# A selective-scan layer: who spreads dt * x, and which operand of each tile's scan lies in PSUM

## The chip, the cores and the metric

The kernel runs on one core of a Trainium2 chip. A core has five engines that run side by side, each with its own queue of instructions that it takes in order: TensorE (PE, matrix multiply, writes to PSUM only), VectorE (DVE, elementwise work and scans), ScalarE (ACT, activations and copies), GpSimd (POOL, here elementwise work in SBUF only), and SyncE (SP, which here issues all DMAs). SBUF is the working memory, PSUM the small memory of eight banks that PE writes. The metric is the device time of one execution of the whole program in microseconds (us), lower is better.

## The reference

The network has four layers. Layers 0, 2 and 3 are deformable convolutions; layer 1 is a "VSS" block, whose core is a two-dimensional selective scan (SS2D) in four directions. Only layer 1 is touched. Cut to its core (B images, K = 4 directions, 256 channels d, 16 states n, L = 56 x 56 positions):

```python
dt = softplus(einsum('bkrl,kdr->bkdl', dts, dt_projs_w) + dt_projs_b)
A = -exp(A_logs).reshape(K, Di, N)
def step(h, t):
    dt_t, u_t, B_t, C_t = t
    h = h * exp(dt_t[..., None] * A) + (dt_t * u_t)[..., None] * B_t[:, :, None, :]
    y = einsum('bkdn,bkn->bkd', h, C_t)
    return (h, y)
_, ys = scan(step, h0, (dt, xs, Bsm, Csm))
```

So for every channel and state there is a recurrence over the positions: the old state times a decay exp(dt * A), plus dt * x * B, and the result weighted with C is summed over the states.

## The kernel before

Layer 1 is the class `Vss`. Its method `scans` takes 8 images x 4 directions x 4 chunks of 784 positions, 128 steps in all. A step has 32 tiles of 128 partitions x 784 positions: a tile holds 32 channels x 4 states on its partitions. Tiles are ordered by channel group `cg` (8 of them) and, inside one, by state group `sg` (4), so four tiles in a row share the channels, and with them dt and dt * x. A step and a tile within it are `at` and `t`; `t % 4` is `sg`. There are 4,096 tiles in all.

For each tile:

- `fetch_dt` (L1286, once for a channel group) and `fetch_row` (L1278) bring dt, dt * x, and the rows of B and C into SBUF by DMA from SP's queue, repeated over the partitions.
- `spread` (L1335, once for a channel group) has PE multiply dt * x with the identity, in two halves of 392 positions, which puts a copy of it into PSUM: the tile `dtu`, two banks, one buffer.
- `decay` (L1343): ACT computes dA = exp(dt * A) into PSUM, two buffers of two banks.
- `inputs` (L1348): u = dt * x * B. For the first three tiles of a group DVE multiplies `dtu` (PSUM) with B (SBUF) into SBUF, tag `u`, two buffers. For the fourth (`on_pool`) POOL does it from SBUF to SBUF, tag `up`.
- L1449: DVE's `tensor_tensor_scan` runs the recurrence over the 784 positions into `h` (SBUF, three buffers); its start value is one column of `st`. For one of its inputs it reads dA in PSUM, for the other u in SBUF.
- L1452: ACT copies the last column of h back into `st` for the next chunk, 32 tiles later (not after the last chunk).
- L1454: POOL multiplies h with C into `hc` (SBUF, six buffers).
- `add_sums` (L1372): PE sums `hc` over the states into `acc` (one PSUM bank), two tiles at a time. `open_sums` (L1364) starts `acc` with the skip term or the running sum over the directions, `close_sums` (L1380) has ACT copy it out (L1389), once for two channel groups.

PSUM's eight banks are `misc` 1, `dtu` 2, dA 4, `acc` 1.

The loop at L1405 walks over the tiles. At tile `now` it emits the decay and the u of tile `now + 1` (the u of a fourth tile one tile earlier), at the second tile of a channel group the spread of the next group (L1442, tile `now + 3`), then the scan, the column copy and POOL's product of tile `now`. Sums are held back: `add_sums` by three tiles, opening and closing by five. Between the tiles `advance` and `ready` emit small pieces of background work: `prepare` (projections, softplus of the next step), `input_stage` (normalization and convolution of the next image) and `output_stage` (norms, gate, MLP of finished rows). They use the single `misc` bank, where PE and ACT take turns.

A planner (the tile framework) assigns the buffers, inserts the waits and orders each engine's queue by its own estimate of when things become ready, so the queue may differ from the order of emission. `issue_after(x)` puts what is emitted inside it behind instruction x on the same engine's queue. Before the change the sums are so tied behind the last spread (L1374).

Of the kernel before, what the change touches and what calls it, by code (L numbers as in the profile page):

```python
# [41 lines left out]
F32 = mybir.dt.float32  # L42
BF16 = mybir.dt.bfloat16
I32 = mybir.dt.int32
AF = mybir.ActivationFunctionType
ALU = mybir.AluOpType
AX = mybir.AxisListType
PSUM = bass.MemoryType.PSUM
# [70 lines left out]
SC, SR = 784, 14  # L119
NSC = L // SC  # L120
SH = SC // 2
# [11 lines left out]
TC, TS = 32, 4  # L133
NCG, NSG = DI // TC, NST // TS
# [342 lines left out]
class Dcn:  # L477
# [9 lines left out]
    def run(self):  # L487
        tc, nc = self.tc, self.nc
        with ExitStack() as ctx:
            enter = ctx.enter_context  # L490
            self.cp = enter(tc.tile_pool(name="c_const", bufs=1))
            self.img = enter(tc.tile_pool(name="c_img", bufs=1))
            self.fp = enter(tc.tile_pool(name="c_front", bufs=1))
            self.up = enter(tc.tile_pool(name="c_unit", bufs=1))
            self.bp = enter(tc.tile_pool(name="c_block", bufs=3))
            self.tp = enter(tc.tile_pool(name="c_tail", bufs=1))
            self.pt = enter(tc.tile_pool(name="c_pt", bufs=3, space=PSUM))
            self.py = enter(tc.tile_pool(name="c_py", bufs=2, space=PSUM))
            self.pm = enter(tc.tile_pool(name="c_pm", bufs=3, space=PSUM))
            self.w = self.net.dcn_weights(self.layer, self.const)  # L500
            self.constants()
            self.split_bias()
            self.loop()
            self.check()
        over = nc.values_load(self.net.flag[:1, :1], min_val=0, max_val=1, skip_runtime_bounds_check_because="a comparison's result")
        with tc.If(over > 0):
            self.net.dcn_slow(self.layer, self.images, self.src, self.dst)
# [482 lines left out]
class Vss:  # L990
# [8 lines left out]
    def run(self):  # L999
        tc = self.tc  # L1000
        with ExitStack() as ctx:
            enter = ctx.enter_context
            self.cp = enter(tc.tile_pool(name="v_const", bufs=1))
            self.img = enter(tc.tile_pool(name="v_img", bufs=1))
            self.prep = enter(tc.tile_pool(name="v_prep", bufs=1))
            self.work = enter(tc.tile_pool(name="v_work", bufs=2))
            self.bg = enter(tc.tile_pool(name="v_bg", bufs=1))
            self.dram = enter(tc.tile_pool(name="v_dram", bufs=2, space=DRAM))
            self.pmisc = enter(tc.tile_pool(name="v_misc", bufs=1, space=PSUM))
            self.pdtu = enter(tc.tile_pool(name="v_pdtu", bufs=1, space=PSUM))  # L1010
            self.pda = enter(tc.tile_pool(name="v_pda", bufs=2, space=PSUM))
            self.pacc = enter(tc.tile_pool(name="v_pacc", bufs=1, space=PSUM))
            self.weights()
            self.scans()
# [285 lines left out]
    def scans(self):  # L1300
        nc, w = self.nc, self.w
# [6 lines left out]
        units = [(at, t) for at in range(len(steps)) for t in range(NT)]  # L1308
# [22 lines left out]
        def on_pool(t):  # L1331

            return order[t][1] == NSG - 1

        def spread(at, t):  # L1335

            s, (cg, sg) = state[at], order[t]
            ps = s["dtu", cg] = self.pdtu.tile([128, 2, 512], F32, name="dtu", tag="dtu")
            for b in range(2):
                last = nc.tensor.matmul(ps[:, b, :SH], lhsT=self.net.ident, rhs=s["dt", cg][:, 1, SH * b : SH * (b + 1)], start=True, stop=True)  # L1340
            self.last_spread = last.ins

        def decay(at, t):  # L1343
            (i, k, c), s, (cg, sg) = steps[at], state[at], order[t]
            da = s["dA", t] = self.pda.tile([128, 1024], F32, name="dA", tag="dA")
            nc.scalar.activation(da[:, :SC], s["dt", cg][:, 0], AF.Exp, scale=w["A"][:, k, NSG * cg + sg : NSG * cg + sg + 1])  # L1346

        def inputs(at, t):  # L1348
            s, (cg, sg) = state[at], order[t]
            if on_pool(t):  # L1350
                u = self.work.tile([128, SC], F32, name="up", tag="up", bufs=1)
                nc.gpsimd.tensor_mul(u, s["dt", cg][:, 1], s["b", sg])  # L1352
            else:
                u = self.work.tile([128, SC], F32, name="u", tag="u", bufs=2)
                halves = [v.rearrange("p (x e) -> p x e", x=2) for v in (u, s["b", sg])]
                nc.vector.tensor_mul(halves[0], s["dtu", cg][:, :, :SH], halves[1])  # L1356
            s["u", t] = u
# [13 lines left out]

        def add_sums(at, group):  # L1372
            acc = state[at]["acc"]
            with self.tc.issue_after(self.last_spread):  # L1374
                for (cg, sg), hc in group:
                    for b in range(2):
                        r = 64 * b + TC * (cg % 2)
                        nc.tensor.matmul(acc[r : r + TC, :SH], lhsT=w["sum"], rhs=hc[:, SH * b : SH * (b + 1)], start=False, stop=sg == NSG - 1)  # L1378

        def close_sums(at, t):  # L1380
            (i, k, c), acc, (h, r) = steps[at], state[at]["acc"], place(t)
# [12 lines left out]
            if t == NT - 1:  # L1394
                state[at] = None
                if k == 2:
                    tasks.extend(self.output_stage(i, e) for e in (2 * c + 1, 2 * c))

        spread(*units[0])
        decay(*units[0])  # L1400
        inputs(*units[0])
        st = ready = None
        group, late = [], deque()
        zeros = self.zeros()
        for now, (at, t) in enumerate(units):  # L1405
            (i, k, c), s, (cg, sg) = steps[at], state[at], order[t]
            forward = k < 2
            if t == 0:
                if at % NSC == 0:
                    st = self.prep.tile([128, NT], F32, name="st", tag="st", bufs=2)  # L1410
                    nc.gpsimd.memset(st, 0.0)
                if at % (NDIR * NSC) == 0 and i + 1 < self.images:
                    tasks.append(self.input_stage(i + 1))
                ready = iter(())
                if at + 1 < len(steps):
                    if steps[at + 1][0] > i:
                        self.load_xb(i + 1)
                    ready = self.prepare(state[at + 1], *steps[at + 1][1:])
            if t % (2 * NSG) == 0:
                late.append((now + 5, open_sums, (at, t)))  # L1420
            while late and late[0][0] <= now:
                _, do, args = late.popleft()
                do(*args)
            if t % 2 == 0:
                next(ready, None)

            if sg == 1:
                to = divmod(NCG * at + cg + 2, NCG)
                if to[0] < len(steps):
                    self.fetch_dt(state[to[0]], to[1])  # L1430
            if t in (3, 19):
                next(zeros, None)

            for x, when in enumerate(((25, 28, 29, 30), (26, 29, 30, 31))):
                if t in when and at + 1 < len(steps):
                    self.fetch_row(state[at + 1], x, when.index(t))
            if now + 1 < len(units):
                decay(*units[now + 1])
                if not on_pool(units[now + 1][1]):
                    inputs(*units[now + 1])  # L1440

                if sg == NSG - 3 and now + 3 < len(units):  # L1442
                    spread(*units[now + 3])
            if now + 2 < len(units) and on_pool(units[now + 2][1]):
                inputs(*units[now + 2])
            hh = self.work.tile([128, SC], F32, name="h", tag="h", bufs=3)
            step = 1 if forward else -1
            u, dA = s.pop(("u", t)), s.pop(("dA", t))
            nc.vector.tensor_tensor_scan(hh[:, ::step], dA[:, :SC][:, ::step], u[:, ::step], st[:, t : t + 1], ALU.mult, ALU.add)  # L1449
            if c != (NSC - 1 if forward else 0):  # L1450
                last = SC - 1 if forward else 0
                nc.scalar.copy(st[:, t : t + 1], hh[:, last : last + 1])  # L1452
            hc = self.work.tile([128, SC], F32, name="hc", tag="hc", bufs=6)
            nc.gpsimd.tensor_mul(hc, hh, s["c", sg])  # L1454
            group.append((order[t], hc))
            if t % 2:
                late.append((now + 3, add_sums, (at, group)))
                group = []
                if t % (2 * NSG) == 2 * NSG - 1:
                    late.append((now + 5, close_sums, (at, t)))  # L1460
            if t % 2 or t % 4 == 0 or (i == self.images - 1 and k == 2):
                advance(1)
# [81 lines left out]
```

## Time and profile before

Three runs took 18473.61, 18480.29 and 18486.9 us, median 18480.29. The profiled execution has a span of 18479.8 us from its first to its last instruction, with a mean granted TensorE clock of 0.826. Its five largest groups of instructions all belong to the scans (busy time and mean length; the idle time of the engine just before them):

| line, engine | what | count | busy us | mean ns | idle before, us |
|---|---|---|---|---|---|
| L1454 POOL | hc = h * C | 4096 | 7560.9 | 1873 | 764.2 |
| L1449 DVE | scan, u made by DVE | 3072 | 5569.9 | 1838 | 316.2 |
| L1449 DVE | scan, u made by POOL | 1024 | 1876.7 | 1833 | 242.4 |
| L1346 ACT | dA = exp(dt * A) | 4096 | 3742.8 | 915 | 719.1 |
| L1378 PE | sums over states | 16384 | 3222.3 | 552 | 105.8 |
| L1356 DVE | u = dtu * B | 3072 | 2875.7 | 957 | 559.9 |
| L1340 PE | dtu = dt * x | 4096 | 2105.1 | 642 | 1512.1 |
| L1352 POOL | u of each fourth tile | 1024 | 1900.3 | 1856 | 132.1 |
| L1452 ACT | column copies | 3072 | 581.7 | 189 | 2159.0 |

How to read it: "busy" is the time of the group's own instructions, "idle before" the time its engine stood still just ahead of them, with no statement that this costs anything. An engine's queue is in order: a waiting instruction holds up everything behind it. PE shows two records for each half of a spread and of a sum, and its ends are modelled. All DMAs are issued by SP.

### The profile page before, as it was taken

To read this page: it belongs to the slowest core of one execution; us is meant where nothing else is said; L and a number is where in the kernel's file an instruction comes from. 1 tells how busy PE (TensorE), PEld (TensorE's weight loads), DVE (VectorE), ACT (ScalarE), POOL (GpSimd) and SP (SyncE) were. 2 spreads that over 40 slices of the span, in tenths; PEclk is the share of its full clock that TensorE was granted. 3 is DMA by queue.
4 is the path that set the end of the run, shared out by engine and by line. 5 is a ranking of instruction groups with operands and counts; after the bars stand their busy time and mean duration, and the time that the engine had idled before them with its cause. 6 is when DMAs were issued, how large, how long until landed. Compare 5 with 4: busy or idle time off the path is not lost. (4 is left out here: it accounts for less than half of the span.)

```text
span 18479.8 us, 257190 instructions
## 1 busy us (share of the span) xinstructions
PE 13780.6 (75%) x89795; PEld 6844.2 (37%) x89795; DVE 15510.8 (84%) x18797; ACT 11145.4 (60%) x20690; POOL 11801.5 (64%) x6462
## 2 busy tenths in 40 slices
PE   5777787678678778678778768767665888577777
PEld 4555422222222222222222222222224666455555
DVE  8888379988988988988988898898985887688886
ACT  4666565566566566566566656656554666456666
POOL 2221089998998998998998998899981111222221
PEclk7878888889889889889888888888886888677777
DMA  7777444444443444344343443443433777577777
GB/s 215 205 210 200 122 158 160 162 158 148 142 149 137 146 147 140 140 150 139 140 150 136 143 152 135 143 150 136 147 122 110 196 198 198 143 204 204 201 204 175
DMA packets 1341779, 2961.90 MB, mean 160 GB/s; under 512 B 91168, under 2 KB 892132, under 8 KB 1325836
## 3 DMA queue, kind: packets, MB, share of 16 engines
q1 hardware_dynamic: 1340460, 2945.21, 51.4%
q8 instruction: 718, 11.76, 0.3%
q14 instruction: 601, 4.92, 0.1%
HBM read 2243.88 MB, written 866.92 MB: 168 GB/s over the span
## 5 line engine op out<-in xcount | busy, mean ns | idle before, releaser
L1454 POOL TENSOR_TENSOR hc<-h,c 128x784 f32<-128x784 f32 x4096 | 7560.9, 1873 | 764.2 <-DVE h L1449 534.4
L1449 DVE TENSOR_TENSOR_SCAN h<-dA,st,u 128x784 f32<-128x784 f32 x3072 | 5569.9, 1838 | 316.2 <-ACT dA L1346 182.3
L1346 ACT ACTIVATE dA<-dt,v_A 128x784 f32<-128x784 f32 x4096 | 3742.8, 915 | 719.1 <-DVE h L1449 717.8
L1356 DVE TENSOR_TENSOR u<-dtu,b 128x784 f32<-128x784 f32 x3072 | 2875.7, 957 | 559.9 <-PE dtu L1340 555.5
L1378 PE MATMUL acc<-hc,v_sum 128*32 128x392 f32 x16384 | 3222.3, 552 | 105.8 <-POOL hc L1454 105.6
L1340 PE MATMUL dtu<-dt,ident 128*128 128x392 f32 x4096 | 2105.1, 642 | 1512.1 <-issue 1102.6
L736 POOL TENSOR_TENSOR ay<-hat,om 112x756 f32<-112x756 f32 (+2 forms) x192 | 525.8, 2738 | 2750.0 <-ACT hat L727 2346.6
L1449 DVE TENSOR_TENSOR_SCAN h<-dA,st,up 128x784 f32<-128x784 f32 x1024 | 1876.7, 1833 | 242.4 <-POOL hc L1454 176.7
L1352 POOL TENSOR_TENSOR up<-dt,b 128x784 f32<-128x784 f32 x1024 | 1900.3, 1856 | 132.1 <-DVE h L1449 110.8
L807 ACT COPY st<-pt 128x448 f32<-128x448 f32 (+1 forms) x2240 | 1177.8, 542 | 1216.4 <-PE pt L805 1210.1
L1452 ACT COPY st<-h 128x1 f32<-128x1 f32 x3072 | 581.7, 189 | 2159.0 <-DVE h L1449 2150.5
L1340 PEld LDWEIGHTS dtu<-dt,ident 128*128 128x128 f32 x4096 | 862.0, 235 | 2564.6 <-issue 1672.2
L775 DVE TENSOR_TENSOR win<-win,patch 112x252 f32 (+2 forms) x3456 | 1695.4, 503 | 124.4 <-DVE win L775 34.2
L805 PE MATMUL pt<-ident,sw 112*128 112x112 f32 (+2 forms) x8960 | 1609.7, 310 | 199.1 <-DMA sw<-skew 198.8
L1378 PEld LDWEIGHTS acc<-hc,v_sum 128*32 128x32 f32 x16384 | 769.8, 117 | 2488.2 <-issue 1675.4
L766 POOL MEMSET win<- 128x1820 f32 (+2 forms) x384 | 630.1, 1646 | 1466.2 <-DMA skew<-win 1159.6
L821 PE MATMUL yps<-st,xw 128*32 128x48 f32 (+5 forms) x35840 | 1077.7, 245 | 397.6 <-ACT st L807 394.8
L805 PEld LDWEIGHTS pt<-ident,sw 112*128 112x128 f32 (+2 forms) x8960 | 1119.5, 161 | 485.6 <-DMA sw<-skew 166.9
L772 DVE TENSOR_TENSOR patch<-ay,hat 112x756 f32<-112x756 f32 (+2 forms) x1152 | 1221.3, 1066 | 22.5 <-POOL ay L736 19.5
L821 PEld LDWEIGHTS yps<-st,xw 128*32 128x32 f32 (+2 forms) x35840 | 757.0, 126 | 825.9 <-ACT st L807 476.1
L1112 PE MATMUL misc<-xn,v_tap 128*128 128x448 f32 x2016 | 867.3, 574 | 96.5 <-ACT xn L1146 61.2
L725 ACT ACTIVATE hat<-om,taps 112x252 f32<-112x252 f32 x1280 | 755.7, 729 | 287.1 <-DVE patch L772 273.4
(165 smaller groups left out, 19517.2 us busy)
## 6 DMA issues: line engine op xcount, KB each, us to landing
dt<-dds SPq DMA_DIRECT2D x1024, 784.0 KB
b<-rows SPq DMA_DIRECT2D x512, 392.0 KB
c<-rows SPq DMA_DIRECT2D x512, 392.0 KB
dds<-dd SPq DMA_DIRECT2D x256, 784.0 KB
sw<-skew SPq DMA_DIRECT2D x224, 812.0 KB
sw<-skew SPq DMA_DIRECT2D x224, 672.0 KB
sw<-skew SPq DMA_DIRECT2D x224, 588.0 KB
xw<-table SPq DMA_DIRECT2D x224, 320.0 KB
```

Source lines behind the costliest of these rows:

```text
L772: nc.vector.tensor_mul(patch[:n], bcast(a, 3, KX), bcast(b, 2, KY))
L775: self.last_add = nc.vector.tensor_add(to, to, patch[:n, NCB * p : NCB * (p + 1)]).ins
L805: last = nc.tensor.transpose(ps[:m, n * g : n * (g + 1)], sw[:n, g, p : p + m], self.net.ident[:n, :n])
L807: nc.scalar.copy(st[:m], ps[:m, : G * n])
L821: self.nc.tensor.matmul(yps[CG * g : CG * (g + 1), t0:t1], lhsT=xw[:m, k + part, CG * g : CG * (g + 1)], rhs=st[:m, at + t0 : at + t1], st ...
L1340: last = nc.tensor.matmul(ps[:, b, :SH], lhsT=self.net.ident, rhs=s["dt", cg][:, 1, SH * b : SH * (b + 1)], start=True, stop=True)
L1346: nc.scalar.activation(da[:, :SC], s["dt", cg][:, 0], AF.Exp, scale=w["A"][:, k, NSG * cg + sg : NSG * cg + sg + 1])
L1352: nc.gpsimd.tensor_mul(u, s["dt", cg][:, 1], s["b", sg])
L1356: nc.vector.tensor_mul(halves[0], s["dtu", cg][:, :, :SH], halves[1])
L1378: nc.tensor.matmul(acc[r : r + TC, :SH], lhsT=w["sum"], rhs=hc[:, SH * b : SH * (b + 1)], start=False, stop=sg == NSG - 1)
L1449: nc.vector.tensor_tensor_scan(hh[:, ::step], dA[:, :SC][:, ::step], u[:, ::step], st[:, t : t + 1], ALU.mult, ALU.add)
L1454: nc.gpsimd.tensor_mul(hc, hh, s["c", sg])
```

## The change

It has six edits, all in `Vss.scans` and its pools but for the last:

1. `spread`: ACT copies dt * x from SBUF to the same PSUM tile, one instruction of 784 elements, in place of PE's identity matmuls.
2. `decay`: the decays of odd tiles go to PSUM with one buffer of two banks (`dAp`), those of even tiles to SBUF with three buffers (`dA`). In the loop an even tile `now` emits the decay of `now + 1`, an odd one that of `now + 3`, so decays of even tiles are emitted two tiles earlier than before.
3. `inputs`: u of even tiles goes to PSUM with one buffer of two banks (`up`, pool `v_pu`), u of odd tiles that DVE makes to SBUF with one buffer instead of two. POOL's u of the fourth tile stays in SBUF (now tag `ug`). The scan of an even tile then reads dA from SBUF and u from PSUM, that of an odd one dA from PSUM and u from SBUF.
4. The sums are no longer tied behind the last spread.
5. The column copy is tied behind the decay or spread emitted last on ACT (`self.ahead`).
6. The scratch of the DMA descriptor ring is set to 8192, half of what it was.

PSUM's banks are then `misc` 1, `dtu` 2, `dAp` 2, `up` 2, `acc` 1.

```diff
-            self.pda = enter(tc.tile_pool(name="v_pda", bufs=2, space=PSUM))
+            self.pda = enter(tc.tile_pool(name="v_pda", bufs=1, space=PSUM))
+            self.pu = enter(tc.tile_pool(name="v_pu", bufs=1, space=PSUM))
...
-            for b in range(2):
-                last = nc.tensor.matmul(ps[:, b, :SH], lhsT=self.net.ident, rhs=s["dt", cg][:, 1, SH * b : SH * (b + 1)], start=True, stop=True)
-            self.last_spread = last.ins
+            self.ahead = nc.scalar.copy(ps[:, :, :SH], s["dt", cg][:, 1].rearrange("p (b e) -> p b e", b=2)).ins
...
-            da = s["dA", t] = self.pda.tile([128, 1024], F32, name="dA", tag="dA")
-            nc.scalar.activation(da[:, :SC], s["dt", cg][:, 0], AF.Exp, scale=w["A"][:, k, NSG * cg + sg : NSG * cg + sg + 1])
+            if t % 2:
+                da = s["dA", t] = self.pda.tile([128, 1024], F32, name="dAp", tag="dAp")[:, :SC]
+            else:
+                da = s["dA", t] = self.work.tile([128, SC], F32, name="dA", tag="dA", bufs=3)
+            self.ahead = nc.scalar.activation(da, s["dt", cg][:, 0], AF.Exp, scale=w["A"][:, k, NSG * cg + sg : NSG * cg + sg + 1]).ins
...
-                u = self.work.tile([128, SC], F32, name="up", tag="up", bufs=1)
+                u = self.work.tile([128, SC], F32, name="ug", tag="ug", bufs=1)
...
-                u = self.work.tile([128, SC], F32, name="u", tag="u", bufs=2)
+                if t % 2:
+                    u = self.work.tile([128, SC], F32, name="u", tag="u", bufs=1)
+                else:
+                    u = self.pu.tile([128, 1024], F32, name="up", tag="up")[:, :SC]
...
-            with self.tc.issue_after(self.last_spread):
...
         decay(*units[0])
+        decay(*units[2])
...
-                decay(*units[now + 1])
+                if t % 2 == 0:
+                    decay(*units[now + 1])
+                elif now + 3 < len(units):
+                    decay(*units[now + 3])
...
-                nc.scalar.copy(st[:, t : t + 1], hh[:, last : last + 1])
+                with self.tc.issue_after(self.ahead):
+                    nc.scalar.copy(st[:, t : t + 1], hh[:, last : last + 1])
...
-    nc = bacc.Bacc("TRN2", target_bir_lowering=False, num_devices=1)
+    nc = bacc.Bacc("TRN2", target_bir_lowering=False, num_devices=1, dynamic_dma_scratch_size=8192)
```

More of the change, by code (lines that the diff above doesn't have):

```diff
@@ L1373, in add_sums @@
             acc = state[at]["acc"]
-            with self.tc.issue_after(self.last_spread):
[L1375 to L1378, printed above, removed]
+            for (cg, sg), hc in group:
+                for b in range(2):
+                    r = 64 * b + TC * (cg % 2)
+                    nc.tensor.matmul(acc[r : r + TC, :SH], lhsT=w["sum"], rhs=hc[:, SH * b : SH * (b + 1)], start=False, stop=sg == NSG - 1)
         def close_sums(at, t):
@@ L1448, in scans @@
             u, dA = s.pop(("u", t)), s.pop(("dA", t))
-            nc.vector.tensor_tensor_scan(hh[:, ::step], dA[:, :SC][:, ::step], u[:, ::step], st[:, t : t + 1], ALU.mult, ALU.add)
+            nc.vector.tensor_tensor_scan(hh[:, ::step], dA[:, ::step], u[:, ::step], st[:, t : t + 1], ALU.mult, ALU.add)
             if c != (NSC - 1 if forward else 0):
                 last = SC - 1 if forward else 0
-                nc.scalar.copy(st[:, t : t + 1], hh[:, last : last + 1])
+                with self.tc.issue_after(self.ahead):
+                    nc.scalar.copy(st[:, t : t + 1], hh[:, last : last + 1])
             hc = self.work.tile([128, SC], F32, name="hc", tag="hc", bufs=6)
```

## The prediction

> **What bounds the kernel now.** I read the slices of the page first, then busy time by stage, then the waits inside the stage that the change touches. The slices (one digit is the busy tenth of 462 us):
>
> ```profile
> DVE  8888379988988988988988898898985887688886
> ACT  4666565566566566566566656656554666456666
> POOL 2221089998998998998998998899981111222221
> ```
>
> POOL is busy only where the scans run (slices 6 to 30). The decay rows of the trace lie between 2359.6 and 13796.9 us, so I cut the span at 2359 and 13801. Columns below: length, then busy us of PE, PE weight loads, DVE, ACT, POOL, the granted clock, the DMA share, GB/s:
>
> ```profile
> 0.00:2359.00 2359.00, 1671.92 (x18091) 1221.27 (x18092) 1661.58 (x3429) 1341.48 (x2510) 411.92 (x244) 0.79 0.68 190
> 2359.00:13801.00 11442.00, 8645.25 (x31311) 3032.12 (x31311) 10266.39 (x8602) 7054.44 (x13031) 10460.49 (x5765) 0.86 0.41 145
> 13801.00:18480.00 4679.00, 3463.46 (x40396) 2590.82 (x40392) 3582.85 (x6766) 2749.52 (x5150) 929.04 (x454) 0.76 0.69 182
> ```
>
> The first and third stage hold none of the edited code: I leave them at 2359 and 4679. In the scan stage (4,096 tiles, so 2.79 us each) POOL is busy 91% and DVE 90%: two engines with the same load, feeding each other. POOL's 10460 us of work is the floor of the stage; 982 us lie above it. What DVE's 1176 idle us wait for:
>
> ```profile
> DVE u L1356 <- PE dtu L1340: 555.5, 259, 82.0
> DVE h L1449 <- ACT dA L1346: 234.3, 199, 4.2
> DVE h L1449 <- POOL hc L1454: 214.4, 165, 3.2
> ```
>
> (waiter, releaser: total us, times, longest.) The 82.0 is the start-up of the stage, before the first u at 2364.11, and stays. So dt * x spread by PE costs DVE 473 us. POOL waits for DVE's scan 645 us (534.4 + 110.8), for PE to free hc 176. DVE's order explains the dtu wait (start, length, operation):
>
> ```profile
> 6018.78 0.95 DVE L1356 TENSOR_TENSOR u<-dtu,b 128x784 f32<-128x784 f32 x1
> 6019.86 1.85 DVE L1449 TENSOR_TENSOR_SCAN h<-dA,st,u 128x784 f32<-128x784 f32 x1
> 6022.57 0.97 DVE L1356 TENSOR_TENSOR u<-dtu,b 128x784 f32<-128x784 f32 x1 [0.86 <-PE dtu L1340]
> ```
>
> The last reader of one dtu ends at 6019.73, one scan follows, and the next u wants the new dtu; PE needs 2.75 us for it in that place (from 6019.78), a scan lasts 1.85.
>
> **The spread goes from PE to ACT.** PE loses 2105 us (row L1340; its loads lie beside it): 8645 to 6540. ACT gains 1,024 copies of 784 elements, SBUF to PSUM, which no row shows. Low end: the decay (915 ns, SBUF to PSUM) less what a per-partition operand costs, 582 for L1265 against 479 for the plain copy L1389 of the same 392 elements, so 103: 812. High end: the exp of L1268, SBUF to SBUF, 855. I take 0.83, the direction of the first: 850 us. Does it sit on the path? It must fit between the last u of a group and the first u of the next. In the first part of the stage DVE's order leaves two scans there (two at 2802.87 and 2805.44, then u at 2807.20), later often one. After the change the first u of a group is in the only PSUM u buffer, free only when the group's third scan ends; today's third u, held by the same kind of release, follows one scan further in every stretch I read. I expect the same for the first u, hence always two scans, 3.6 us, against 0.83. What is late then is ACT itself. Today 4,096 decays with about 2.8 us of slack (a u of 0.95 and a scan of 1.84 lie between the scan that frees a dA buffer and the one that needs it again) cost 234 us, 57 ns each; 1,024 copies at half as much again cost 90. So 473 goes, 90 comes. If the cover were one scan, slack is 1.0 us: last rival.
>
> **Decays.** Even ones (2,048) go to SBUF: 855 + 103 = 958 against 915, 43 ns each, 88 us on ACT. Two tiles ahead of the old place with three buffers, they no longer wait for a scan just ended; their half of the 234 nearly goes. Odd ones keep a PSUM buffer that the previous odd scan frees, the same two-tile distance as today; their 117 grows with ACT's load (7054 + 850 + 88 = 7992 us, of 11050 that is 72%, today 62%) to perhaps 160. Sum 180 for 234: 54 us off. An earlier decay needs its dt earlier, but no earlier than the spread at the same tile does today, and no L1340 row waits for a DMA: nothing.
>
> **u.** 2,048 of the 3,072 multiplies write PSUM instead of SBUF, and their scans read dA from SBUF and u from PSUM, still one of each. No DVE row writes PSUM. By the nearest rows the side matters little: bn_stats from PSUM is 416 ns for 256 elements, 149 above 256 / 0.96; from SBUF 270 for 128, 137 above. That is 12 ns: 25 us in all. Against the change speaks the Trainium skill, "Perfetto Trace Analysis", section Optimizing Scalar/DVE Operations: an access overhead of about 60 ns for DVE on SBUF, 125 on PSUM; by its 65 ns an estimate of 133 us. Both are added DVE work, on the path. I take the row, 25, and keep 0 and 133 as ends; below 0 is excluded, as DVE has no row that is shorter for PSUM.
>
> **Column copies.** Today copy and next decay are released by the same scan and the copy goes first (decay begins 0.10 us after it, 6001.61 and 6001.71). Tied behind, the decay gains 0.1. The copy is then behind a decay or a spread. Behind it wait ACT's next work and the h buffer; h has three, its other reader on POOL takes 1.87 us, so a copy 0.9 later is covered. The column itself is read 32 tiles later. If the tied copy waits long (a spread waiting for its u), h is late and DVE waits: part of the last rival. Net nothing.
>
> **PE's sums** lose their tie to the spread and 2105 us ahead of them. POOL's 176 us for hc and ACT's waits on PE (402.0 + 132.5 + 229.1 + 159.9 + 155.2 + 101.8 = 1180 us) should shrink; I halve the 176.
>
> **DMA ring.** All issues of the trace stand on SP, and the queues are
>
> ```profile
> q1 hardware_dynamic: 1340460, 2945.21, 51.4%
> q8 instruction: 718, 11.76, 0.3%
> q14 instruction: 601, 4.92, 0.1%
> ```
>
> No POOL DMA exists for a smaller ring to hold up: nothing, unless the profile after shows one. SBUF needs 6,272 bytes more per partition (three dA less one u, 3,136 each).
>
> **The sum, two ways.** DVE's own waits: -473 + 90 - 54 + 25 = -412, and more waiting for POOL. The windows tell how much: at 2700:3500 the dtu wait is only 16.7 us in 800, DVE waits for hc about 2.8% of the time (1.9% over the stage), 100 us more over 11,400: -312. POOL's view:
>
> ```profile
> 2700.00:3500.00 800.00, 539.69 (x1905) 163.49 (x1903) 743.55 (x535) 436.21 (x759) 768.30 (x426) 0.84 0.44 156
> ```
>
> Here, with the dtu wait small, POOL is busy 96%. But no output stage runs in it and ACT has 55%. With the change the stage should come near it, not reach it: 10460 / 0.945 = 11070, -372; at 0.96 it would be -546. Half of POOL's hc wait, 88 us, speaks for the second way. I take -400: 18479.8 to **18080 us**. The median of the runs (18480.3) is the same as the span to 0.5 us, so it carries over.
>
> **Rivals.**
> (a) POOL takes it all back: the dtu wait turns into waits for hc, since POOL has 2% more work than DVE. For it: the pairs of 0.7 to 2.4 us before scans at 2805 and 2827. Against: 645 of POOL's idle us are DVE's fault. If only a quarter of 473 comes through plus 54: about -170, 18310. With the 133 of PSUM writes at full price and the rest as forecast: 18190.
> (b) No effect: the edits cancel, 18480. Little speaks for it.
> (c) Slower: **ACT becomes late once a group**. If the spread stands ahead of the fourth tile's decay in ACT's queue, the chain is third u, spread 0.83, column copy 0.1, decay 0.91, together 1.84, against one scan of 1.84 that covers it. Then everything else on ACT counts: its other work (7054 - 3743 - 582 = 2729 us, 2.7 per group of 10.9) puts 0.5 us into such a 2 us window, its waits on PE (1180) 0.2. That is 0.7 us a group, 720 us, less 473: +250, 18730. It decides from 0.46 us per group on. Against: a decay is ready at the scan's end, 0.95 us before the spread, and an order by readiness puts it first.
>
> **Chances.** Forecast (17930 to 18250) 0.56; (a) 0.14; (b) 0.06; (c) 0.24. About 0.2% (37 us) can be told from no change. Faster 0.70, same 0.06, slower 0.24. Range: low end POOL at 96% (17930); high end into (c), leaving out its worse half: 18620.
>
> **What the profile after would show.** Right: no PE dtu row, DVE's wait for dtu (now by ACT) near 90 us plus start-up, dA wait below 200, hc wait above 214, POOL at 94 to 96% of a stage near 11050, u multiplies of 0.95 to 0.97, DVE's order with two scans between the last u of a group and the next. Wrong: multiplies into PSUM above 1.0 us, or DVE waiting for ACT more than 470 us in sum, or a stage longer than 11442.

## The result and the profile after

The changed kernel takes 18609.26 us (median of 4 runs, 18591.79 to 18618.9) against 18481.81 for the kernel before on the same chip: ratio 1.0069, 95% interval 1.0055 to 1.0084. It is slower by 0.7%, where 18080 us and faster was forecast. The time lies inside the stated range (17930 to 18620 us) only because the range's high end was taken from rival (c). The span of the profiled execution is 18590.1 us.

The stages of the profile after, cut at the same 2359 us and at a round time just past its last scan (columns as before: length, busy us of PE, PE weight loads, DVE, ACT, POOL, granted clock, DMA share, GB/s):

```profile
0.00:2359.00 2359.00, 1677.77 (x18093) 1223.59 (x18093) 1665.12 (x3430) 1343.18 (x2512) 410.58 (x245) 0.79 0.69 190
2359.00:13920.00 11561.00, 8140.76 (x27231) 2288.17 (x27230) 10303.97 (x8606) 7787.86 (x14064) 10462.15 (x5766) 0.76 0.41 144
13920.00:18600.00 4680.00, 3461.37 (x40376) 2592.85 (x40376) 3586.89 (x6762) 2743.21 (x5140) 925.65 (x452) 0.76 0.69 182
```

First and third stage stand still. The scan stage takes it all: its last sum ends at 13914 us instead of 13804. POOL does the same work as before (10462 us busy) and DVE 38 us more (10304), so most of what grew is waiting. ACT has 733 us more to do, PE only 504 less, and PE's granted clock in this stage fell from 0.86 to 0.76. What DVE waits for in the scan stage now (waiter, releaser: total us, times, longest):

```profile
DVE h L1457 <- ACT dAp L1348: 356.3, 248, 6.1
DVE up L1361 <- ACT dtu L1340: 285.7, 128, 8.8
DVE bn_st L1070 <- PE misc L1174: 150.3, 45, 9.5
DVE h L1457 <- ACT st L1461: 105.3, 35, 5.8
DVE h L1457 <- POOL hc L1463: 104.3, 138, 2.8
DVE up L1361 <- DMA dt<-dds: 78.5, 1, 78.5
DVE xt L1228 <- PE misc L1225: 73.3, 31, 5.8
```

The 78.5 is the start-up. The old wait for dtu (473 us) shrank by 187; the wait for POOL's h buffers by 110. Against them, decays +122, column copies +93, PE's background results (bn_st and xt) +180, with a longest wait of 9.5 us for bn_st where it was 2.6 before. Two of the prediction's signs of being wrong are there: DVE waits for ACT 751 us in sum (more than 470), and the stage is longer than 11442 us. Something held PE and ACT for a long time now and then. The waits of PE and ACT name it; before the change:

```profile
PE acc L1378 <- POOL hc L1454: 105.6, 124, 2.0
...
ACT y L1389 <- PE acc L1378: 402.0, 237, 7.4
ACT sp L1265 <- PE misc L1264: 229.1, 202, 3.5
...
ACT dbl L1253 <- PE misc L1251: 155.2, 117, 5.4
```

After it:

```profile
PE acc L1382 <- POOL hc L1463: 2079.9, 1682, 7.3
```

```profile
ACT y L1393 <- PE acc L1382: 548.7, 206, 7.0
...
ACT sp L1266 <- PE misc L1265: 350.8, 232, 7.3
ACT dbl L1254 <- PE misc L1252: 326.2, 130, 9.0
```

PE's sums stood 105.6 us for hc before, now 2080. ACT's waits for PE, summed over all its rows of this view, rose from 1289 to 1885 us. Counted from starts and ends in the two traces, the first sum of a tile begins a median 7.3 us after its hc is done before the change and 0.3 us after it now: the sums stand in PE's queue right where their input is made. One place of the timeline shows how this reaches DVE (start, length, operation, idle time before it and what ended it):

```profile
6002.93 5.33 PE L1382 MATMUL acc<-hc,v_sum 128*32 128x392 f32 x18
...
6003.36 1.82 DVE L1457 TENSOR_TENSOR_SCAN h<-dA,st,up 128x784 f32<-128x784 f32 x1
...
6008.30 3.73 POOL L1463 TENSOR_TENSOR hc<-h,c 128x784 f32<-128x784 f32 x2
...
6010.24 0.85 PE L1382 MATMUL acc<-hc,v_sum 128*32 128x392 f32 x4 [1.99 <-POOL hc L1463]
...
6012.08 1.52 PE L1382 MATMUL acc<-hc,v_sum 128*32 128x392 f32 x4 [0.99 <-POOL hc L1463]
...
6013.54 1.09 PE L1174 MATMUL misc<-ident,yin 128*98 128x128 f32 x4
6014.66 0.76 DVE L1070 BATCH_NORM_STATS2 bn_st<-misc 98x6 f32<-98x256 f32 x2 [9.48 <-PE misc L1174]
...
6018.34 1.85 POOL L1463 TENSOR_TENSOR hc<-h,c 128x784 f32<-128x784 f32 x1 [6.31 <-DVE h L1457]
```

POOL is late with hc. PE has a run of sums in its queue (four records to a tile), and behind them stands a background transpose. DVE has the statistics of that transpose ahead of its next u and scan and waits 9.48 us from the end of its scan at 6005.18: some 3 us of it pass while PE works on sums that stand ahead, another 3 us (1.99 and 0.99) while PE stands still for hc. Then POOL has no h and waits 6.31 us. POOL's lag goes round through PE and DVE and comes back to POOL.

### The profile page after: what moved, and what is told of

It is laid out like the page before. It is cut to its first block, busy times and chain, and to the rows that moved or that the text cites. A ratio compares the mean times of both kernels' runs of the same rounds, so it can differ in the third digit from the quotient of the medians.

```text
span 18590.1 us, 248627 instructions
## 1 busy us (share of the span) xinstructions
PE 13279.9 (71%) x85699; PEld 6104.6 (33%) x85699; DVE 15556.0 (84%) x18797; ACT 11874.3 (64%) x21714; POOL 11798.4 (63%) x6462
## 3 DMA queue, kind: packets, MB, share of 16 engines
q1 hardware_dynamic: 1340460, 2945.21, 51.3%
## 5 line engine op out<-in xcount | busy, mean ns | idle before, releaser
L1382 PE MATMUL acc<-hc,v_sum 128*32 128x392 f32 x16384 | 4361.7, 634 | 2102.3 <-POOL hc L1463 2079.9
L1457 DVE TENSOR_TENSOR_SCAN h<-dA,st,up 128x784 f32<-128x784 f32 x2048 | 3764.8, 1838 | 104.6 <-ACT st L1461 26.3
L1361 DVE TENSOR_TENSOR up<-dtu,b 128x784 f32<-128x784 f32 x2048 | 1978.2, 966 | 393.4 <-ACT dtu L1340 285.7
L1457 DVE TENSOR_TENSOR_SCAN h<-dAp,st,ug 128x784 f32<-128x784 f32 x1024 | 1881.0, 1837 | 321.7 <-ACT dAp L1348 244.7
L1348 ACT ACTIVATE dAp<-dt,v_A 128x784 f32<-128x784 f32 x2048 | 1871.4, 914 | 353.8 <-DVE h L1457 352.4
L1457 DVE TENSOR_TENSOR_SCAN h<-dAp,st,u 128x784 f32<-128x784 f32 x1024 | 1877.5, 1833 | 226.3 <-ACT dAp L1348 111.7
L1348 ACT ACTIVATE dA<-dt,v_A 128x784 f32<-128x784 f32 x2048 | 1924.4, 945 | 208.3 <-DVE h L1457 195.1
L1354 POOL TENSOR_TENSOR ug<-dt,b 128x784 f32<-128x784 f32 x1024 | 1900.9, 1856 | 59.9 <-DVE h L1457 42.9
L1361 DVE TENSOR_TENSOR u<-dtu,b 128x784 f32<-128x784 f32 x1024 | 984.4, 961 | 0.0
```

The source lines that it names most:

```text
L1348: self.ahead = nc.scalar.activation(da, s["dt", cg][:, 0], AF.Exp, scale=w["A"][:, k, NSG * cg + sg : NSG * cg + sg + 1]).ins
L1457: nc.vector.tensor_tensor_scan(hh[:, ::step], dA[:, ::step], u[:, ::step], st[:, t : t + 1], ALU.mult, ALU.add)
```

## The experiments

Times are medians; each ratio is to the kernel before, timed beside it, with its 95% interval.

**First question: which part of the change costs?** Four theories: (1) PE lost work, so its granted clock fell and its hand-offs to ACT got slower; (2) ACT has too much in its queue; (3) the tied column copies hold the h buffers; (4), formed after the first four runs, the untied sums block PE.

*PE makes the spread again, the sums are tied behind it, the rest as changed:*

```diff
-            self.ahead = nc.scalar.copy(ps[:, :, :SH], s["dt", cg][:, 1].rearrange("p (b e) -> p b e", b=2)).ins
+            for b in range(2):
+                last = nc.tensor.matmul(ps[:, b, :SH], lhsT=self.net.ident, rhs=s["dt", cg][:, 1, SH * b : SH * (b + 1)], start=True, stop=True)
+            self.last_spread = last.ins
...
+            with self.tc.issue_after(self.last_spread):
```

> The changed kernel with PE's identity matmuls for dt * x again and the sums tied behind them; decays, u and column copies as changed. Theory 1 (without the identity matmuls PE's granted clock in the scan stage falls, 0.86 to 0.76, and PE-ACT hand-offs of the background work get slower and hold up ACT): clock back at 0.84 or more, ACT's waits on PE back from 1879 us to about 1300, time about 18400. Theory 2 (ACT is overloaded by 1,024 copies in its queue): the same time, and ACT's load back at 62 to 63%. Theory 3 (the tied column copies hold h): stays at 18580 or more.

Measured: 18429.06 us, ratio 0.9973 (0.9962 to 0.9984), clock of the scan stage 0.86, ACT's waits on PE 1344 us. The rest of the change (placing of decays and u, tied copies, smaller ring) helps a little; theory 3 falls; 1 and 2 both remain.

*The kernel before with only the spread moved to ACT and the sums untied:*

```diff
-            for b in range(2):
-                last = nc.tensor.matmul(ps[:, b, :SH], lhsT=self.net.ident, rhs=s["dt", cg][:, 1, SH * b : SH * (b + 1)], start=True, stop=True)
-            self.last_spread = last.ins
+            self.ahead = nc.scalar.copy(ps[:, :, :SH], s["dt", cg][:, 1].rearrange("p (b e) -> p b e", b=2)).ins
...
-            with self.tc.issue_after(self.last_spread):
```

> The kernel before with only the spread moved to ACT and the sums untied. Theories 1 and 2: slower than before, 18550 to 18700, clock near 0.76, DVE's waits for ACT's dA above 300 us. Theory 3 (the tied copies are what costs): faster than before, about 18300, since DVE's 473 us of waits for dtu go and nothing is tied.

Measured: 18697.22 us, ratio 1.0119 (1.0103 to 1.0136), clock 0.76, DVE's waits for dA 690 us. The loss is in these two edits, and they alone lose more than the whole change.

*The changed kernel with the column copies not tied:*

```diff
-                with self.tc.issue_after(self.ahead):
-                    nc.scalar.copy(st[:, t : t + 1], hh[:, last : last + 1])
+                nc.scalar.copy(st[:, t : t + 1], hh[:, last : last + 1])
```

> The changed kernel with the column copies not tied. Theory 3: DVE's waits for ACT's column copies (105 us) go, time 18500 or less. Theories 1 and 2: 18600 within 40 us, clock 0.76.

Measured: 18630.33 us, ratio 1.0080 (1.0063 to 1.0097). DVE still waits 83 us for column copies: they are late with or without the tie. Theory 3 falls again.

*The changed kernel with PE kept busy:*

```diff
+            (cg, sg), hc = group[0]
+            for b in range(2):
+                r = 64 * b + TC * (cg % 2)
+                nc.tensor.matmul(acc[r : r + TC, :SH], lhsT=w["nought"], rhs=w["in"][:, :SH], start=False, stop=False)
             for (cg, sg), hc in group:
```

> The changed kernel with two more matmuls on PE before each pair of tiles is summed (weights of zero, added into acc, 4,096 instructions in all, about twice the removed identity matmuls). Theory 1: clock of the scan stage 0.84 or more, PE's background matmuls as short as before (L1264 at 573 ns), time 18500 or less. Theory 2 or 3: clock up, time 18600 or more, since PE has more to do and ACT and its copies are unchanged.

Measured: 18683.11 us, ratio 1.0109 (1.0092 to 1.0126). The clock is back at 0.85 and the background matmul of `prepare` (L1264 before the change) at 609 ns (664 in the changed kernel, 573 before), and yet ACT's waits on PE are 1920 us and the time is worse. A faster clock with the same queue did not bring the time back; the added work is in this number too.

In this kernel, as in the changed one, PE stands at the sums (1554 us for hc). That led to theory 4: before the change each spread stood in PE's queue until DVE had read the old dtu, and the sums were tied behind it. So they came after an event of the scan, when most hc were done, and other matmuls could be ahead of them.

**Second question: is it the tie?**

*The kernel before with this one edit, the sums untied:*

```diff
-            with self.tc.issue_after(self.last_spread):
-                for (cg, sg), hc in group:
+            for (cg, sg), hc in group:
```

> The kernel before with one edit alone: the sums no longer tied behind the spread; PE still makes the spread. Theory 4 (the tie kept PE from standing at a sum whose hc is not there yet; untied sums block PE's queue, so the background matmuls, and ACT behind them, come late): slower than before by 100 us or more, 18580 to 18750, PE waiting for POOL's hc thousands of us as in the changed kernel, ACT's waits on PE near 1850 us, clock still 0.84 or more. Theory 2 (ACT's load): no change, 18480 within 40 us.

Measured: 19399.7 us, ratio 1.0496 (1.0479 to 1.0514), the dearest of all edits, and far dearer than was expected. The clock is 0.85, ACT's load unchanged. PE's spread now stands behind the blocked sums too, which the changed kernel with its spread on ACT is spared, so the loss here is no measure of the loss there. The first rows of DVE's waits and PE's largest group in the scan stage:

```profile
DVE u L1356 <- PE dtu L1340: 1446.0, 645, 80.6
DVE h L1448 <- ACT dA L1346: 327.3, 251, 4.7
```

```profile
L1377 PE MATMUL acc<-hc,v_sum 128*32 128x392 f32 x16384 | 4124.5, 577 | 1849.3 <-POOL hc L1453 1842.6 <-DMA dt<-dds 0.5 <-DMA skew<-zeros 0.3
```

(the last columns: busy us, mean ns, idle before and its releasers.) Without the tie PE waits 1843 us for hc with the clock up and nothing added to ACT.

*The changed kernel with the sums tied again.* PE has no spread any more, so a matmul of two columns into unused columns of `acc` stands in for it; it reads h of the group's second tile:

```diff
+            if sg == 1 and self.acc_now is not None:
+                self.mark = nc.tensor.matmul(self.acc_now[TC : 2 * TC, SH : SH + 2], lhsT=w["sum"], rhs=hh[:, :2], start=False, stop=False).ins
...
+            with self.tc.issue_after(self.mark) if self.mark is not None else nullcontext():
```

(`acc_now` is the `acc` opened last.)

> The changed kernel with the sums tied again, behind a small matmul (two columns, into unused columns of acc) that reads h of the second tile of the group, so that it runs at about the time of the old spread. Theory 4: PE's wait for hc falls below 1000 us, ACT's waits on PE to about 1350 us, time 18430 or less, although the clock stays near 0.76. Theory 2 (ACT's load): stays above 18550. Theory 1 (clock): 18600.

Measured: 18296.92 us, ratio 0.9897 (0.9880 to 0.9913): from 0.7% slower to 1.0% faster by a matmul whose result nobody reads, at a clock of 0.78. PE waits 319 us for hc, ACT 1290 for PE. PE stands still for h and hc nearly as long as it stood for hc in the changed kernel (1752 us against 2080), only elsewhere:

```profile
PE acc L1465 <- DVE h L1459: 1433.0, 580, 8.8
...
PE acc L1383 <- POOL hc L1467: 318.8, 324, 2.8
```

L1465 is the small matmul. The kernel before stood 1512 us ahead of its spreads (381 of them for DVE's u, 1103 for nothing that the profile shows). So it is not PE's standing still by itself that costs; it matters what stands behind. Theories 1 and 2, which expected more than 18550 us here, fall as the main cause. DVE's waits:

```profile
DVE h L1459 <- ACT dAp L1348: 213.9, 168, 6.2
DVE h L1459 <- POOL hc L1467: 185.7, 216, 3.8
DVE up L1361 <- ACT dtu L1340: 182.3, 78, 5.4
...
DVE h L1459 <- ACT st L1463: 47.8, 29, 4.1
```

The waits for ACT fell when the sums were tied again (decays 356 to 214, dtu 286 to 182, column copies 105 to 48), though ACT does the same work. That also speaks against ACT's load as the main cause.

*The same tie in the kernel before with only the spread on ACT:*

```diff
+            nc.scalar.copy(ps[:, :, :SH], s["dt", cg][:, 1].rearrange("p (b e) -> p b e", b=2))
...
-            with self.tc.issue_after(self.last_spread):
+            with self.tc.issue_after(self.mark) if self.mark is not None else nullcontext():
```

> The kernel before with the spread on ACT and the sums tied behind the same small matmul. Theory 4: most of the 218 us that the spread on ACT with untied sums cost goes, time 18400 to 18520. Theory 2: ACT's decays stay late (over 500 us of DVE's waits for dA), 18650 or more.

Measured: 18351.1 us, ratio 0.9929 (0.9913 to 0.9946): 346 us less than without the tie. DVE's waits for dA, 690 us, are 340. The spread on ACT with the small matmul as the tie is thus a gain of about 130 us on the kernel before.

*PE's spread, tied sums, column copies not tied (the same edit as above, on the first experiment's kernel):*

```diff
-                with self.tc.issue_after(self.ahead):
-                    nc.scalar.copy(st[:, t : t + 1], hh[:, last : last + 1])
+                nc.scalar.copy(st[:, t : t + 1], hh[:, last : last + 1])
```

> The kernel with PE's spread and tied sums (18429 us) without the tie of the column copies: decays and u placed as changed, nothing else. If the early decays make the gain of 50 us: 18430 within 20. If the tied copies make it: 18480.

Measured: 18405.71 us, ratio 0.9956 (0.9940 to 0.9973). The placing of decays and u makes the gain (the smaller ring is in it too); the tied copies take some 20 us of it, at the edge of what can be told, since the two intervals overlap.

**Third question: what in the tie works?** The changed kernel with the sums emitted one tile later:

```diff
-                late.append((now + 3, add_sums, (at, group)))
+                late.append((now + 4, add_sums, (at, group)))
```

> The changed kernel with the untied sums emitted four tiles behind their scans instead of three, no small matmul. Theory 4 in its plain form (the sums stand too early in PE's queue): PE's wait for hc falls from 2080 us to about half, time below 18500. If it is the real wait on an event of the scan that matters, and not the place in the plan: 18580 or more.

Measured: 18620.61 us, ratio 1.0077 (1.0061 to 1.0094), PE's wait for hc 2075 us, as in the changed kernel. The place in the program does nothing, but it hardly reached the queue: counted in the traces, 97% of PE's 8,790 background matmul records have exactly as many sums ahead of them as in the changed kernel. What sums that stand later in the queue would do, this run does not tell.

The last run takes the event out of the small matmul and leaves the tie:

```diff
-                self.mark = nc.tensor.matmul(self.acc_now[TC : 2 * TC, SH : SH + 2], lhsT=w["sum"], rhs=hh[:, :2], start=False, stop=False).ins
+                self.mark = nc.tensor.matmul(self.acc_now[TC : 2 * TC, SH : SH + 2], lhsT=w["sum"], rhs=w["in"][:, :2], start=False, stop=False).ins
```

> The kernel with the small matmul (18297 us), which reads a constant instead of h, so that it waits for nothing; the sums are still tied behind it. If the tie works through the event that the small matmul waits for (a scan's end): PE's waits for hc and ACT's waits on PE are as in the changed kernel (2080 and 1885 us), time 18600 within 40. If only the place that the tie gives the sums in PE's queue matters: 18300 within 40.

Measured: 18590.07 us, ratio 1.0056 (1.0040 to 1.0073); PE waits 2030 us for hc, ACT 1869 for PE. The dependence on h is what works, not the tie in itself. It can work by the wait on the chip, or because the planner, which sees it too, then places other matmuls ahead of the sums. The traces show that the order changes: with the small matmul 61% of the background records have fewer sums ahead of them than in the changed kernel (8% have more), a mean of 4.4 records or one tile; without its h 97% stand as in the changed kernel. When the kernel before was untied, 72% had more sums ahead, a mean of 8.4 records. A wait in PE's queue lets nothing past it, as the place at 6010 us above shows, which speaks for the order. But ACT's queue is rearranged with it (38% of ACT's instructions stand in another place), and no run here gives the order without the wait, so their shares stay open.

*Small matmul, column copies not tied (the same edit on that kernel):*

```diff
-                with self.tc.issue_after(self.ahead):
-                    nc.scalar.copy(st[:, t : t + 1], hh[:, last : last + 1])
+                nc.scalar.copy(st[:, t : t + 1], hh[:, last : last + 1])
```

> The kernel with the small matmul (18297 us) without the tie of the column copies. If the tied copies cost as they did beside PE's spread (23 us): 18270. If they help as they did in the changed kernel (21 us): 18320.

Measured: 18253.81 us, ratio 0.9882 (0.9865 to 0.9898). The best of all versions, 1.2% below the kernel before; the tied copies seem to cost here too (43 us, though these two intervals overlap as well).

*Small matmul made eight of 120 columns:*

```diff
-                self.mark = nc.tensor.matmul(self.acc_now[TC : 2 * TC, SH : SH + 2], lhsT=w["sum"], rhs=hh[:, :2], start=False, stop=False).ins
+                for _ in range(8):
+                    self.mark = nc.tensor.matmul(self.acc_now[TC : 2 * TC, SH : SH + 120], lhsT=w["sum"], rhs=hh[:, :120], start=False, stop=False).ins
```

> The kernel with the small matmul, which is now eight matmuls of 120 columns, so that PE has work at that place again. Theory 1 in what is left of it (the granted clock of 0.78 still costs): clock 0.82 or more, PE's background matmuls shorter, time 18250 or less. If the clock is without weight here: 18300 within 30.

Measured: 18825.29 us, ratio 1.0188 (1.0171 to 1.0205); neither expectation held. The clock rose to 0.86, PE's matmuls got shorter (sums 553 ns for 628), and the time rose by 528 us: the eight matmuls, 2479 us in all, stand in the queue ahead of others, and ACT's waits on PE are 2002 us. What the clock alone is worth stays open, since in both trials it came with work; but the two best versions run at 0.78 and 0.79.

All runs in one table (scan stage of the profiled execution; ACT's waits on PE summed over its rows):

| kernel | time, us | clock | PE's sums wait for hc, us | ACT waits for PE, us |
|---|---|---|---|---|
| small matmul, copies not tied | 18254 | 0.79 | 316 | 1228 |
| small matmul | 18297 | 0.78 | 319 | 1290 |
| before, ACT spread, small matmul | 18351 | 0.78 | 280 | 1115 |
| PE spread, copies not tied | 18406 | 0.86 | 126 | 1355 |
| PE spread | 18429 | 0.86 | 124 | 1344 |
| before | 18482 | 0.86 | 106 | 1289 |
| small matmul without h | 18590 | 0.76 | 2030 | 1869 |
| changed kernel | 18609 | 0.76 | 2080 | 1885 |
| later sums | 18621 | 0.76 | 2075 | 1902 |
| copies not tied | 18630 | 0.76 | 2050 | 1876 |
| changed, PE kept busy | 18683 | 0.85 | 1554 | 1920 |
| before, ACT spread, untied | 18697 | 0.76 | 1939 | 1782 |
| small matmul made large | 18825 | 0.86 | 124 | 2002 |
| before, untied | 19400 | 0.85 | 1843 | 2265 |

The last column sorts faster from slower: every version from 1115 to 1355 us is at the kernel before or faster, every one from 1782 up is slower; inside the two groups it does not give the order. The clock and the copies' tie sort nothing, and the wait for hc fails at the large matmul, where other work stands in ACT's way.

## Why the prediction was wrong, step by step

- **PE's sums: the step that failed.** It read: "PE's sums lose their tie to the spread and 2105 us ahead of them. POOL's 176 us for hc and ACT's waits on PE [...] should shrink". POOL's wait for `acc` did shrink (176 to 60), but ACT's waits on PE rose by 596 us. I had costed the removed tie as freedom for the sums and never asked what stands behind them in PE's queue when hc is late, with POOL the fuller of two full engines. The runs show that the sums moved ahead of the background matmuls: PE stood 2080 us for hc (106 before), and ACT and DVE got their background results late. With a stand-in for the tie, the whole change is faster by 1.0%.
- **The copy on ACT**: sized right (812 ns measured, 0.83 taken). The place was less right than thought: in the early stretch two scans do lie between the last u of a group and the next first u, as forecast:

```profile
2814.63 1.85 DVE L1457 TENSOR_TENSOR_SCAN h<-dA,st,up 128x784 f32<-128x784 f32 x1
2816.39 1.83 DVE L1457 TENSOR_TENSOR_SCAN h<-dAp,st,ug 128x784 f32<-128x784 f32 x1
2818.14 0.96 DVE L1361 TENSOR_TENSOR up<-dtu,b 128x784 f32<-128x784 f32 x1
```

  Counted over the trace, two scans lie there in 843 of 1,023 groups, three in 33 and one in 147, not "always two". DVE's wait for dtu was 286 us instead of 90, and 166 us of it fall where two scans cover. In the kernel with the small matmul it is 182, so the term was also mis-sized by half.
- **Decays**: 945 ns into SBUF (958 taken). Even decays are never late (1 us of DVE's waits), as forecast. The odd ones cost 356 us where 160 was expected; 214 with the small matmul.
- **u in PSUM**: 966 ns against 961 for the tiles still written to SBUF, 5 ns where the rows gave 12, and the overheads in the Trainium skill ("Perfetto Trace Analysis", section Optimizing Scalar/DVE Operations: about 60 ns on SBUF, 125 on PSUM) gave an estimate of 65. The measurement decides for the rows; DVE's busy time rose 38 us in all, where 25 was taken. The rate in the rows' sum, 0.96 elements a nanosecond, comes out of the trace (L616: 684 ns for 512 elements, 550 for 384). A closer pair was at hand: bn_stats of 128 elements, 276 ns from PSUM (L888) and 271 from SBUF (L1069), 5 ns apart.
- **Column copies**: forecast at nothing. DVE waits 105 us for them, but most of it comes without the tie too (83). Where the sums are tied, the copies' tie costs some 20 to 40 us, at the edge of what can be told.
- **DMA ring**: no POOL DMA in the profile after; its queue of data is the same 1,340,460 packets on SP's queue. Nothing, though the edit was not tried by itself.
- **The two sums** were both made from gains in DVE's and POOL's waits. POOL, forecast at 94.5% of the stage, was busy 90.5%. The forecast of -400 was too large even for the right mechanism: with the small matmul the changed kernel gains 188 us (18484.6 to 18296.9), and POOL is busy 10424 of 11261 us, 92.6%.
- **The rivals**: (c) named the right sign and the right place, ACT late for the fourth tile's scan. The waits of that scan before and after:

```profile
L1449 DVE TENSOR_TENSOR_SCAN h<-dA,st,up 128x784 f32<-128x784 f32 x1024 | 1876.7, 1833 | 242.4 <-POOL hc L1454 176.7 <-ACT dA L1346 52.0 <-ACT st L1452 10.5
...
L1457 DVE TENSOR_TENSOR_SCAN h<-dAp,st,ug 128x784 f32<-128x784 f32 x1024 | 1881.0, 1837 | 321.7 <-ACT dAp L1348 244.7 <-POOL hc L1463 55.9 <-POOL ug L1354 15.3
```

  The order that (c) blamed first is there: the spread stands ahead of the fourth decay in 427 of 1,023 groups. But only 75 of the 245 us fall in these groups. With the small matmul 135 us remain, nearly all of them in such groups (132 us in 422). So the order inside ACT's queue has a cost of its own, and the larger part in the changed kernel came from elsewhere: from ACT's waits on PE, which (c) put at 0.2 us a group, as before the change, and which were the part that grew.

## What to carry to other kernels

A tie or a wait in an in-order queue may be what keeps a late producer from stopping everyone behind it. Before one is removed, ask what stands behind the freed instruction when its input is late, and whose time that is; here the dependence of a two-column matmul is worth 293 us (18590 against 18297). When a step is moved off an engine, look for what else hung on it: the spread was also the signal behind which the sums were held.

## What the runs showed that was not expected

PE's granted clock went with how much PE had to do, not with how long it stood still: the kernel before with untied sums has 0.85 with the spread on PE and 0.76 with the spread on ACT, and PE stands over 1800 us for hc in both. Removing 2105 us of matmuls from an 11,400 us stage took the changed kernel from 0.86 to 0.76, and the sums grew from 552 to 634 ns each, so that PE's busy time fell by 504 us only. That holds for this stage's work; the third stage has 0.76 with PE busy 74% of the time, where the scan stage before had 0.86 with 76%. Adding work brought the clock back (0.85 and 0.86) but never the time.
